# Normalisation stage of a four-layer image kernel: another order of its products, squares taken from PSUM, eight kept pieces spread out, the last three pieces left in SBUF

## The chip, the cores and the metric

The kernel runs on 1 core of one Trainium2 chip. The metric is the device time of one execution in microseconds (us). The engines are named as in the profile: PE (TensorE matmul), PEld (its weight loads), DVE (VectorE), ACT (ScalarE), POOL (GpSimd), SP (SyncE, which here only issues transfers). SBUF is the working memory, PSUM the memory that PE writes its products to, DRAM the large memory outside.

## The reference, cut to what matters

An image `x` of 256 x 256 pixels with 128 channels goes through four layers, each of the form `x = x + layer(group_norm(x))`. Only the first layer is touched by the change: row attention over the image, with a layer norm in front and a bias that is shared by all rows.

```
def _L0_conv_ref(z, ln_scale, ln_bias, Wq, Wk, Wv, Wb, Wg, Wo):      # z = _gn(x)
    mu = jnp.mean(z, axis=-1, keepdims=True)
    var = jnp.mean(jnp.square(z - mu), axis=-1, keepdims=True)
    zn = (z - mu) * jax.lax.rsqrt(var + EPS) * ln_scale + ln_bias
    q, k, v = zn @ Wq, zn @ Wk, zn @ Wv        # 4 heads of 32
    bias = zn @ Wb
    g = jax.nn.sigmoid(zn @ Wg)
    scores = jnp.einsum('bijhd,bikhd->bijkh', q, k) * (1.0 / C ** 0.5)
    scores = scores + bias[:, None, :, :, :]
    a = jax.nn.softmax(scores, axis=-2)
    o = jnp.einsum('bijkh,bikhd->bijhd', a, v)
    return (g * o).reshape(b, n, n, H * C) @ Wo
```

The other three layers (a recurrence in the frequency plane, a triangle product, a convolution) follow, and take the time from about 1660 us to the end.

## The kernel before, in words

All data is 32-bit. The image is worked on in 32 pieces of 2048 pixels (1 MB, eight image rows each), and attention in 128 row pairs of 512 pixels (`rp`), four to a piece. Three stages matter here:

**Statistics** (`statistics`, 0 to about 126 us). Every piece is read once, pixels on partitions, to sum `x` and its squares for the group norm. The last seven pieces read, which are pieces 0 to 6, go to tiles of their own (`kept`) and stay in SBUF.

**Normalisation** (`attention`, about 132 to 445 us). The group norm and the centring of the layer norm are folded into one matrix `lc` and one column `cb`. For each piece `m`:

- `turn(m)`: sixteen PE transposes (`pt`) put channels on partitions; ACT copies the first half and DVE the second half into `xo`, and POOL issues its write to DRAM (`xT`). `load(m + 2)` reads a piece that was not kept from DRAM again (`xin`), issued by SP.
- `centre(m, b)` for both halves `b`: two products `zc` (L60), a DVE addition of `cb` into `zs`, and ACT's square `sq` of `zs`.
- `variance(m)`: four products `var` with weights of 32 columns, so that each fills one of four strips of 32 partitions; ACT's logarithm and exponential make `rs`, one over the standard deviation.
- `normalise(m)`: four products `pr` spread `rs` over all channels (each uses a strip of 32 rows of PE); DVE multiplies `zs` by them into `zn`; POOL applies scale and bias and issues the write to DRAM (`znT`).
- `pair_bias(m)`: four products `pbias` make the bias of the piece's pixels; DVE copies it (`bi`), and SP issues four writes to DRAM (`biasD`). `load_bias` reads it back in another layout (`bias`).

The order on the engines is the program's (`tc.keep_in_program_order`), and every engine works its queue in order. One turn of the loop is: `turn(m+1)`, `variance(m)`, first half of `centre(m+1)`, `normalise(m)`, `pair_bias(m-1)`, second half of `centre(m+1)`. Of PSUM's eight banks, six hold three wide buffers of two banks, which `pt`, `zc` and `pr` share in turn, and two hold two row buffers, which `var` and `pbias` share in turn. A write to a buffer waits until its last reader is done. The weights of the later layers (`later_weights`) and the first row transforms (`row_transforms`, tile `hs`) are SP transfers of this stage too.

**Attention** (`attend_bounded`, about 445 to 1660 us). Ahead of its loop stand the projections `q`, `k`, `g`, `v` of the first two row pairs, the transposes of the bias (`pbt`, copied to `bT`), and the scores `sc` of the first two rows. In one turn, for row pair `rp`: POOL's folds `ks`, scores of the next pair, DVE's addition of the bias (`e`), ACT's exponentials, the four projections of pair `rp + 2`, the products `nd` of the exponentials with `v`, and the output `px`. `zn` and `x` of a row pair are read from DRAM by `chunk`; those of pairs 0 and 1 were read early into `first`. A second way, `attend_any`, stands behind a test of the weights and isn't taken.

Of the kernel before, what the change touches and what calls it, by code (L numbers as in the profile page):

```python
# [9 lines left out]
F32 = mybir.dt.float32  # L10
AF = mybir.ActivationFunctionType
ALU = mybir.AluOpType
# [5 lines left out]
P = 128  # L18
N = 256
NPIX = N * N  # L20
NCH = NPIX // 512
NH, HD = 4, 32
KS = 7
HC = P // 2
LN_EPS = 1e-5
LN_EXP = "natural_log_exp_and_others"
# [4 lines left out]
class Kernel:  # L31
# [27 lines left out]
    def mm(self, out, lhsT, rhs, start=True, stop=True):  # L59
        return self.nc.tensor.matmul(out, lhsT, rhs, start=start, stop=stop)  # L60
# [144 lines left out]
    def statistics(self, wp, weights, HD_, kept, src):  # L205
# [3 lines left out]
        nc, I = self.nc, self.i  # L209
        V = nc.vector  # L210
        x = I["x"].rearrange("b h w c -> (b h w) c")
        NM, KEPT = NPIX // 2048, len(kept)
        mv = wp.tile([P, 2], F32, name="mvx")
        with ExitStack() as c:
            sp = c.enter_context(self.pool(name="sp", bufs=1))
# [21 lines left out]
                                    start=count[j] < 2, stop=count[j] >= 4 * NM - 2)  # L237
                            count[j] += 1

            order = list(range(KEPT, NM)) + list(range(KEPT))  # L240
            spectrum, made = None, 0
            for n, m in enumerate(order):
                if m < KEPT:
                    xin = kept[m]
                else:
                    xin = io.tile([P, 2, 1024], F32, name="xin", bufs=3)
                nc.sync.dma_start(xin, src(m))
                for b in range(2):
                    xs = io.tile([P, 1024], F32, name="xs")
                    pin(V.tensor_tensor)(xs.rearrange("p (t c) -> p t c", t=8), xin[:, b].rearrange("p (t c) -> p t c", t=8),  # L250
                                    sh.unsqueeze(1).to_broadcast([P, 8, P]), ALU.subtract)
                    sq = io.tile([P, 1024], F32, name="sqx")
                    pin(self.act)(sq, xs, AF.Square)

                    add_up(xs, last)
# [91 lines left out]
    def attention(self, wp, later, xT, x1T, znT, biasD, HD_, stats1, shift1):  # L347
# [5 lines left out]
        with ExitStack() as c:  # L353

            bias = wp.tile([P, 2, NH, N], F32, name="bias")
            first = tuple(wp.tile([P, 1024], F32, name=n) for n in ("zn0", "xr0"))
            c1 = c.enter_context(ExitStack())
            kp = c1.enter_context(self.pool(name="kp", bufs=1))

            kept = [kp.tile([P, 2, 1024], F32, name=f"kept{m}") for m in range(7)]  # L360
            mv, (w, (lns, lnb), wo, small) = self.statistics(wp, self.attention_weights(wp), HD_, kept, src)
            with self.pool(name="awq", bufs=2, space=PSUM) as ps0:
                ab, mg, _ = self.group_affine(wp, ps0, None, self.g4, "0", True, mv=mv)
# [11 lines left out]

            io = c1.enter_context(self.pool(name="a1", bufs=3))
            work = c1.enter_context(self.pool(name="a1w", bufs=3))
            ps = c1.enter_context(self.pool(name="a1s", bufs=3, space=PSUM))  # L380
# [4 lines left out]
            pin = lambda f: lambda *a, **k: tc.keep_in_program_order(f(*a, **k))  # L385
            mm, act, tt, ts, copy = pin(self.mm), pin(self.act), pin(V.tensor_tensor), pin(V.tensor_scalar_add), pin(V.tensor_copy)
            transpose, acopy = pin(nc.tensor.transpose), pin(nc.scalar.copy)
            xin, xo, zn, sq, zs, rs, var, spreads = dict(enumerate(kept)), {}, {}, {}, {}, {}, {}, {}
            wide = lambda name: ps.tile([P, 1024], F32, name=name, tag="w")
            row = lambda name: ps.tile([P, 512], F32, name=name, tag="r", bufs=2)  # L390

            def load(m):
                if m < NM and m not in xin:
                    xin[m] = io.tile([P, 2, 1024], F32, name="xin")
                    nc.sync.dma_start(xin[m], src(m))

            def turn(m):
                if m >= NM:
                    return
                load(m + 2)  # L400
                xo[m] = io.tile([P, 2, P, 8], F32, name="xo")
                for b in range(2):
                    pt = wide("pt").rearrange("c (t p) -> c t p", t=8)
                    for t in range(8):
                        transpose(pt[:, t], xin[m][:, b, t * P:(t + 1) * P], self.ident)
                    (copy if b else acopy)(xo[m][:, b], pt.rearrange("c t p -> c p t"))
                nc.gpsimd.dma_start(xT[:, m * 2048:(m + 1) * 2048], xo[m].rearrange("c b p t -> c (b p t)"))

            def centre(m, b):
                if m >= NM:  # L410
                    return
                zc = wide("zc")
                for k in range(2):
                    mm(zc[:, k * 512:(k + 1) * 512], lc, xo[m][:, b].rearrange("c p t -> c (p t)")[:, k * 512:(k + 1) * 512])
                zs[m, b] = work.tile([P, 1024], F32, name="zs")
                ts(zs[m, b], zc, cb)
                sq[m, b] = work.tile([P, 1024], F32, name="sq")
                act(sq[m, b], zs[m, b], AF.Square)

            def variance(m):  # L420
                var = row("var")
# [4 lines left out]
                act(rs[m], rs[m], AF.Exp, scale=-0.5)  # L426

            def normalise(m):
                zn[m] = io.tile([P, 2048], F32, name="zn")
                pr = [wide("pr") for _ in range(2)]  # L430
                for k in range(4):
                    mm(pr[k // 2][:, (k % 2) * 512:(k % 2 + 1) * 512], spread[32 * k:32 * k + 32], rs[m][32 * k:32 * k + 32])
                for b in range(2):
                    z = zn[m][:, b * 1024:(b + 1) * 1024]
                    tt(z, zs[m, b], pr[b], ALU.mult)
                    nc.gpsimd.tensor_scalar(z, z, lns, lnb, ALU.mult, ALU.add)
                nc.gpsimd.dma_start(znT[:, m * 2048:(m + 1) * 2048], zn[m])

            def pair_bias(m):
                if m < 0:  # L440
# [8 lines left out]
                    nc.sync.dma_start(biasD[:, s:s + 512], bi[32 * k:32 * k + NH])  # L449

            tc.keep_in_program_order(self.table(LN_EXP))
            for m in range(7, 9):
                load(m)
            turn(0)
            centre(0, 0)
            centre(0, 1)
            for m in range(NM):
                turn(m + 1)
                variance(m)
                centre(m + 1, 0)  # L460
                normalise(m)
                pair_bias(m - 1)
                centre(m + 1, 1)
                if m == 5:
                    self.later_weights(later)
                elif m == 12:
                    self.first_rows = self.row_transforms(later.tile([P, 2, HC], F32, name="hs0"), HD_, 0)
                elif m == NM - 4:
                    load_bias(0, 192)
                    nc.sync.dma_start(first[0], znT[:, :1024])  # L470
                    nc.sync.dma_start(first[1], xT[:, :1024])
                elif m == NM - 1:
                    load_bias(192, 240)
            pair_bias(NM - 1)
            load_bias(240, 256)
            c1.close()

            flag = nc.values_load(small[0:1, 0:1])
            self.last = {}
            with tc.If(flag > 0) as branch:  # L480
                self.attend_bounded(xT, x1T, znT, bias, first, w, wo, stats1, shift1)
            self.last = {}
            with branch.Else():
                self.attend_any(xT, x1T, znT, bias, w, wo, stats1, shift1)
            self.last = {}

    def bounded(self, wp, raws, w, wb, m32):
# [62 lines left out]
            V.tensor_copy(fl, top[:, 1:2])  # L550
            return fl

    def attend_bounded(self, xT, x1T, znT, bias, first, w, wo, stats1, shift1):


        nc, tc = self.nc, self.tc
# [1 line left out]
        with ExitStack() as c:  # L558
# [17 lines left out]
            pin = lambda f: lambda *a, **k: tc.keep_in_program_order(f(*a, **k))  # L576
            mm, act_t, act_i = pin(self.mm), pin(act), pin(self.act)
            tt, stt, add = pin(V.tensor_tensor), pin(V.scalar_tensor_tensor), pin(nc.gpsimd.tensor_tensor)
            loaded, t, e, es, ks, nd, dn, og, x1s = {0: first}, {}, {}, {}, {}, {}, {}, {}, {}

            def chunk(rp):
# [12 lines left out]
            def project(rp, nm):  # L594
                if rp >= N // 2:
                    return
                z = chunk(rp)[0]
                o = pj.tile([P, 4, P] if nm == "v" else [P, 512], F32, name="t" + nm)
                if nm == "v":
                    pv = ps.tile([P, 4, P], F32, name="ppv", tag="pj")  # L600
                    for ch in range(4):
# [2 lines left out]
                else:  # L604
# [7 lines left out]
                t[rp, nm] = o  # L612

            def score(i):

# [59 lines left out]
            def output(rp):  # L675
# [8 lines left out]
                mm(px, wo["f"], og[rp])  # L684
                stt(x1[:, s], px, 1.0, xr, ALU.mult, ALU.add, accum_out=stats1[:, 0, rp:rp + 1])
                if rp % 2 == 1:
                    nc.gpsimd.dma_start(x1T[:, (rp - 1) * 512:(rp + 1) * 512], x1)

            def squares(rp):
                if rp >= 0:  # L690
# [58 lines left out]
            output(rp)  # L749
            squares(rp)  # L750

    def attend_any(self, xT, x1T, znT, bias, w, wo, stats1, shift1):

        nc, tc = self.nc, self.tc
        with ExitStack() as c:
            io = c.enter_context(self.pool(name="a2", bufs=2))
            pj = c.enter_context(self.pool(name="a2w", bufs=2))
# [842 lines left out]
```

## Time and profile before

| what | us |
|---|---|
| three runs | 4891.92, 4894.64, 4895.0 |
| median | 4894.64 |
| the profiled execution's own time | 4892.94 |
| its span | 4891.1 |

| engine | busy us | share of the span |
|---|---|---|
| PE | 4713.9 | 96% |
| DVE | 3631.1 | 74% |
| ACT | 3327.7 | 68% |
| POOL | 1859.5 | 38% |

| group in the normalisation stage | mean of one, ns |
|---|---|
| DVE addition `zs<-zc`, 128x1024 | 1278 |
| DVE multiplication `zn<-zs,pr`, 128x1024 | 1211 |
| ACT square `sq<-zs`, 128x1024 | 1057 |
| ACT copy `xo<-pt`, 128x1024 | 994 |
| DVE copy `xo<-pt`, 128x1024 | 1225 |
| DVE copy `bi<-pbias`, 128x512 | 682 |
| POOL scale and bias `zn<-zn`, 128x1024 | 1191 |

The second table is the page's first part, the third is from the groups of instructions between 148.7 and 425.3 us. A row of the order of time begins with its start and its length in us; a bracket at its end tells how long the engine had been idle and what ended that. One 32-bit product is two MATMUL instructions, and rows of the same kind that follow each other are merged, with their count behind an x; the ends of matmuls are modelled, so their starts are the surer numbers.

### The profile page before, as it was taken

The numbers are of one execution on the slowest core, as the hardware profiler recorded it, in microseconds if no ns is written. First come the engines' busy times: TensorE is split into PE (matmuls) and PEld (weight loads), VectorE is DVE, ScalarE is ACT, GpSimd is POOL, SyncE is SP. The second block draws the span as 40 slices with busy tenths as digits, with TensorE's granted clock in tenths as the row PEclk, the third lists the DMA queues.
The fourth block names the chain that finished last, engine by engine and source line by source line (L and its number), as shares of the span: only waits on it lengthen the run. The fifth ranks groups of instructions, "written<-read, shape, count | busy, mean of one in ns | idle before, by whom it ended". The sixth has DMA issues, their size and how long they took to land.

```text
span 4891.1 us, 78322 instructions
## 1 busy us (share of the span) xinstructions
PE 4713.9 (96%) x30415; PEld 2672.1 (55%) x30415; DVE 3631.1 (74%) x4551; ACT 3327.7 (68%) x5009; POOL 1859.5 (38%) x1296
## 2 busy tenths in 40 slices
PE   8999999999999899999999997999999999999999
PEld 2444555555555433333333332269999943369999
DVE  6666777777777699999999996763443357789886
ACT  6445888888888799999999995543333367762110
POOL 0333555555555466666666664421001100000000
PEclk9999999999999999999999998999999999999999
DMA  8795222222222245555555555996876688854432
GB/s 300 279 337 211 83 83 87 83 83 85 81 87 83 86 94 134 131 134 133 131 133 133 131 131 144 333 328 224 276 246 226 220 333 326 326 204 166 142 123 70
DMA packets 223923, 848.77 MB, mean 174 GB/s; under 512 B 59351, under 2 KB 62701, under 8 KB 174245
## 3 DMA queue, kind: packets, MB, share of 16 engines
q1 hardware_dynamic: 146638, 505.57, 31.0%
q0 software_dynamic: 75616, 337.76, 23.6%
q8 instruction: 244, 4.00, 0.3%
q14 instruction: 129, 1.05, 0.1%
q10 hardware_dynamic: 1296, 0.40, 0.0%
HBM read 505.18 MB, written 271.32 MB: 159 GB/s over the span
## 4 chain that ended last, share of the span: by engine, by line
PE 59%; ACT 14%; DVE 10%; issue 5%; POOL 1%; DMA 1%; POOLq 0%; ACTq 0%; DVEq 0%
PE z L60 9%; PE m L60 8%; PE nd L60 7%; PE sc L60 6%; PE zc L60 5%; PE po L60 5%; PE ppq L60 3%; PE ppv L60 3%; PE pe L60 2%; PE px L60 2%; PE py L60 2%; PE ppk L60 2%; PE ppg L60 2%; ACT L905 2%; ACT x2q L54 2%
## 5 line engine op out<-in xcount | busy, mean ns | idle before, releaser
L576 DVE TENSOR_TENSOR e<-sc,bT 128x1024 f32<-128x1024 f32 x512 | 613.2, 1219 | 259.0 <-PE sc L60 256.0
L576 POOL TENSOR_TENSOR ks<-e 128x1024 f32<-128x1024 f32 x256 | 601.7, 2371 | 448.6 <-PE nd L60 430.7
L54 ACT ACTIVATE e<-e 128x1024 f32<-128x1024 f32 x512 | 538.8, 1052 | 38.5 <-DVE e L576 29.1
L1091 DVE TENSOR_TENSOR LR<-z,sg 128x512 f32<-128x512 f32 x256 | 268.5, 1049 | 362.5 <-ACT sg L54 362.5
L60 PE MATMUL m<-U,v 128*128 128x128 f32 x4608 | 514.8, 275 | 0.0
L60 PEld LDWEIGHTS m<-U,v 128*128 128x128 f32 x4608 | 514.6, 192 | 0.0
L60 PE MATMUL z<-wf,zt 128*128 128x128 f32 x4096 | 458.4, 275 | 2.1 <-DVE zn L1091 1.4
L60 PEld LDWEIGHTS z<-wf,zt 128*128 128x128 f32 x4096 | 458.0, 192 | 3.3 <-DVE zn L1091 2.2
L54 ACT ACTIVATE sg<-z 128x512 f32<-128x512 f32 x256 | 152.9, 597 | 307.3 <-PE z L60 307.3
L54 ACT ACTIVATE sq<-zs 128x1024 f32<-128x1024 f32 x192 | 202.4, 1054 | 192.4 <-DVE zs L385 156.1
L1223 POOL DMA_DIRECT2D prodD<-o x128 | 69.3, 542 | 616.7 <-ACT o L54 609.2
L60 PE MATMUL sc<-tq,tk 32*128 32x256 f32 x4096 | 298.4, 403 | 2.8 <-DVE e L576 1.9
L933 POOL TENSOR_TENSOR fs<-f 128x512 f32<-128x512 f32 x64 | 176.5, 2759 | 275.7 <-DVE f L930 256.2
L60 PEld LDWEIGHTS sc<-tq,tk 32*128 32x128 f32 x4096 | 187.3, 185 | 160.0 <-PE px L60 94.8
L60 PE MATMUL nd<-e,tv 128*32 128x256 f32 x4096 | 271.3, 382 | 2.5 <-DVE og L576 2.5
L54 ACT ACTIVATE dn<-dn 128x512 f32<-128x512 f32 x384 | 237.9, 619 | 8.0 <-DVE dn L576 3.9
L933 POOL TENSOR_TENSOR u<-t,tr 128x512 f32<-128x512 f32 x64 | 229.6, 3588 | 11.9 <-DVE tr L936 9.9
L933 POOL TENSOR_TENSOR t<-t,v 128x1024 f32<-128x1024 f32 x64 | 209.6, 3275 | 52.5 <-DVE t L930 51.8
L60 PE MATMUL po<-LR 128*128 128x256 f32 x1024 | 222.1, 379 | 7.0 <-DVE LR L1091 7.0
L1476 ACT COPY m4s<-m 128x512 f32<-128x512 f32 x32 | 18.7, 584 | 287.2 <-PE m L60 287.2
L60 PEld LDWEIGHTS po<-LR 128*128 128x128 f32 x1024 | 194.2, 190 | 34.0 <-DVE LR L1091 7.7
L1486 POOL DMA_DIRECT2D out_dram<-ys x32 | 37.0, 1156 | 423.9 <-DVE ys L1484 412.0
(377 smaller groups left out, 10670.7 us busy)
## 6 DMA issues: line engine op xcount, KB each, us to landing
zt<-znT SPq DMA_DIRECT2D x128, 1024.0 KB
znT<-zn POOLq DMA_DIRECT2D x64, 1024.0 KB, 5.1
xin<-x2T SPq DMA_DIRECT2D x64, 1024.0 KB
xin<-in_x_dram SPq DMA_DIRECT2D x50, 1024.0 KB
xr<-x3T SPq DMA_DIRECT2D x46, 768.0 KB
xT<-xo POOLq DMA_DIRECT2D x32, 1024.0 KB, 9.4
xr<-xT SPq DMA_DIRECT2D x64, 512.0 KB
zn<-znT SPq DMA_DIRECT2D x64, 512.0 KB
```

Source lines behind the costliest of these rows:

```text
L54: return self.nc.scalar.activation(out, in_, func, bias=bias, scale=scale, **kw)
L60: return self.nc.tensor.matmul(out, lhsT, rhs, start=start, stop=stop)
L576: pin = lambda f: lambda *a, **k: tc.keep_in_program_order(f(*a, **k))
L905: pin(nc.scalar.preload_act_table_set(want))
L933: pin(nc.gpsimd.tensor_tensor(out, a, b_, op))
L1091: pin = lambda f: lambda *a, **k: tc.keep_in_program_order(f(*a, **k))
L1223: nc.gpsimd.dma_start(prodD[g * CQ + d].rearrange("(p a j) -> p a j", p=P, a=2), o.rearrange("p a j b -> p a (j b)"))
L1476: nc.scalar.copy(m4, m[4])
L1486: nc.gpsimd.dma_start(out[row:row + 8].rearrange("r p t c -> p (r t) c"), ys.rearrange("p g k t c -> p (g k t) c"))
```

## The change

- **Order of the products.** A turn of the loop is now `variance(m)`, `centre(m+1)` with both halves, `normalise(m)`, `pair_bias(m-1)`, `turn(m+2)`. Two pieces are transposed ahead of the loop.
- **Squares.** ACT squares `zc + cb` straight from PSUM (`bias=cb`); DVE's addition comes after it in the program and writes into `zn`, which is then multiplied in place. `zs` goes.
- **Kept pieces.** Eight pieces, 0, 4, 8, ... 28, stay in SBUF instead of seven, 0 to 6. The other 24 are read again, three ahead, in buffers (`qp`) that stand in their own region.
- **Last three pieces.** `zn` and `xo` of pieces 29, 30 and 31 aren't written to DRAM; attention starts with their twelve row pairs (`turns`). The projections of the first three row pairs are made in the end of the normalisation stage, in the row buffers of PSUM (`project`), and kept in tiles (`early`) which the loop then uses for its own projections in turn. `first` goes.

```diff
-            kept = [kp.tile([P, 2, 1024], F32, name=f"kept{m}") for m in range(7)]
+            kept = {m: kp.tile([P, 2, 1024], F32, name=f"kept{m}") for m in range(0, 32, 4)}
...
+            zp = c.enter_context(self.pool(name="a0", bufs=3, side="right"))
+            yp = c.enter_context(self.pool(name="ay", bufs=4, side="right"))
+            qp = c.enter_context(self.pool(name="aq", bufs=3, side="right"))
...
             def turn(m):
                 if m >= NM:
                     return
-                load(m + 2)
-                xo[m] = io.tile([P, 2, P, 8], F32, name="xo")
+                xo[m] = zp.tile([P, 2, P, 8], F32, name="xo")
...
-                nc.gpsimd.dma_start(xT[:, m * 2048:(m + 1) * 2048], xo[m].rearrange("c b p t -> c (b p t)"))
+                if m not in kept:
+                    load()
+                if m < NM - HELD:
+                    nc.gpsimd.dma_start(xT[:, m * 2048:(m + 1) * 2048], xo[m].rearrange("c b p t -> c (b p t)"))

-            def centre(m, b):
+            def centre(m):
                 if m >= NM:
                     return
-                zc = wide("zc")
-                for k in range(2):
-                    mm(zc[:, k * 512:(k + 1) * 512], lc, xo[m][:, b].rearrange("c p t -> c (p t)")[:, k * 512:(k + 1) * 512])
-                zs[m, b] = work.tile([P, 1024], F32, name="zs")
-                ts(zs[m, b], zc, cb)
-                sq[m, b] = work.tile([P, 1024], F32, name="sq")
-                act(sq[m, b], zs[m, b], AF.Square)
+                zn[m] = yp.tile([P, 2048], F32, name="zn")
+                for b in range(2):
+                    zc = wide("zc")
+                    for k in range(2):
+                        mm(zc[:, k * 512:(k + 1) * 512], lc, xo[m][:, b].rearrange("c p t -> c (p t)")[:, k * 512:(k + 1) * 512])
+                    sq[m, b] = work.tile([P, 1024], F32, name="sq")
+                    act(sq[m, b], zc, AF.Square, bias=cb)
+                    ts(zn[m][:, b * 1024:(b + 1) * 1024], zc, cb)
...
-                    tt(z, zs[m, b], pr[b], ALU.mult)
+                    tt(z, z, pr[b], ALU.mult)
                     nc.gpsimd.tensor_scalar(z, z, lns, lnb, ALU.mult, ALU.add)
-                nc.gpsimd.dma_start(znT[:, m * 2048:(m + 1) * 2048], zn[m])
+                if m < NM - HELD:
+                    nc.gpsimd.dma_start(znT[:, m * 2048:(m + 1) * 2048], zn[m])
...
-            for m in range(7, 9):
-                load(m)
+            for _ in range(3):
+                load()
             turn(0)
-            centre(0, 0)
-            centre(0, 1)
+            turn(1)
+            centre(0)
+            early = {}
+
+            def project(n, names):
+                if n not in early:
+                    early[n] = qp.tile([P, 4, 512], F32, name="proj", tag="xin")
+                z = zn[NM - HELD][:, n * 512:(n + 1) * 512]
+                for nm in names:
+                    pp, o = row("pp" + nm), early[n][:, "qkvg".index(nm)]
...
             for m in range(NM):
-                turn(m + 1)
                 variance(m)
-                centre(m + 1, 0)
+                centre(m + 1)
+                if m == NM - 1:
+                    project(0, "qkvg")
                 normalise(m)
                 pair_bias(m - 1)
-                centre(m + 1, 1)
+                turn(m + 2)
...
-                    nc.sync.dma_start(first[0], znT[:, :1024])
-                    nc.sync.dma_start(first[1], xT[:, :1024])
...
+            project(1, "qkvg")
             pair_bias(NM - 1)
             load_bias(240, 256)
+            project(2, "qkvg")
...
+            turns = [*range(N // 2 - 4 * HELD, N // 2), *range(N // 2 - 4 * HELD)]
+
+            def chunk(n):
+
+                rp = turns[n]
+                if rp // 4 in held:
+                    return tuple(x[:, rp % 4 * 512:(rp % 4 + 1) * 512] for x in held[rp // 4])
...
             def project(rp, nm):
                 if rp >= N // 2:
                     return
+                done = rp in early
+                o = early[rp % len(early)][:, "qkvg".index(nm)]
+                if nm == "v":
+                    o = o.rearrange("p (a b) -> p a b", b=P)
+                t[rp, nm] = o
+                if done:
+                    return
```

`HELD` is 3. In the built program of the changed kernel DVE's addition of a half waits for ACT's square of the same half, and the second `pr` half waits for the addition of the first `zc` half of the piece after it.

More of the change, by code (lines that the diff above doesn't have):

```diff
@@ L23 @@
 KS = 7
+HELD = 3
 HC = P // 2
@@ L211, in statistics @@
         x = I["x"].rearrange("b h w c -> (b h w) c")
-        NM, KEPT = NPIX // 2048, len(kept)
+        NM = NPIX // 2048
         mv = wp.tile([P, 2], F32, name="mvx")
@@ L238, in add_up @@
                             count[j] += 1
-            order = list(range(KEPT, NM)) + list(range(KEPT))
+            order = [m for m in range(NM) if m not in kept] + sorted(kept)
             spectrum, made = None, 0
             for n, m in enumerate(order):
-                if m < KEPT:
+                if m in kept:
                     xin = kept[m]
@@ L355, in attention @@
             bias = wp.tile([P, 2, NH, N], F32, name="bias")
-            first = tuple(wp.tile([P, 1024], F32, name=n) for n in ("zn0", "xr0"))
             c1 = c.enter_context(ExitStack())
             kp = c1.enter_context(self.pool(name="kp", bufs=1))
-            kept = [kp.tile([P, 2, 1024], F32, name=f"kept{m}") for m in range(7)]
+            kept = {m: kp.tile([P, 2, 1024], F32, name=f"kept{m}") for m in range(0, 32, 4)}
             mv, (w, (lns, lnb), wo, small) = self.statistics(wp, self.attention_weights(wp), HD_, kept, src)
@@ L387, in attention, with load @@
             transpose, acopy = pin(nc.tensor.transpose), pin(nc.scalar.copy)
-            xin, xo, zn, sq, zs, rs, var, spreads = dict(enumerate(kept)), {}, {}, {}, {}, {}, {}, {}
+            xin, xo, zn, sq, rs = dict(kept), {}, {}, {}, {}
             wide = lambda name: ps.tile([P, 1024], F32, name=name, tag="w")
             row = lambda name: ps.tile([P, 512], F32, name=name, tag="r", bufs=2)
-            def load(m):
-                if m < NM and m not in xin:
-                    xin[m] = io.tile([P, 2, 1024], F32, name="xin")
+            again = [m for m in range(NM) if m not in kept]
+            def load():
+                if again:
+                    m = again.pop(0)
+                    xin[m] = qp.tile([P, 2, 1024], F32, name="xin")
                     nc.sync.dma_start(xin[m], src(m))
@@ L428, in normalise @@
             def normalise(m):
-                zn[m] = io.tile([P, 2048], F32, name="zn")
                 pr = [wide("pr") for _ in range(2)]
@@ L451, in attention @@
             tc.keep_in_program_order(self.table(LN_EXP))
-            for m in range(7, 9):
-                load(m)
+            for _ in range(3):
+                load()
             turn(0)
-            centre(0, 0)
-            centre(0, 1)
+            turn(1)
[8 more added lines that the diff above has]
+                    if nm == "v":
+                        for ch in range(4):
+                            mm(pp[:, ch * P:(ch + 1) * P], z[:, ch * P:(ch + 1) * P], w["v"])
+                    else:
+                        mm(pp, w[nm], z)
+                    if nm == "g":
+                        act(o, pp, AF.Exp, scale=-1.0)
+                    else:
+                        act(o, pp, AF.Identity)
             for m in range(NM):
-                turn(m + 1)
                 variance(m)
-                centre(m + 1, 0)
+                centre(m + 1)
+                if m == NM - 1:
+                    project(0, "qkvg")
                 normalise(m)
                 pair_bias(m - 1)
-                centre(m + 1, 1)
+                turn(m + 2)
                 if m == 5:
@@ L469, in attention @@
                     load_bias(0, 192)
-                    nc.sync.dma_start(first[0], znT[:, :1024])
-                    nc.sync.dma_start(first[1], xT[:, :1024])
                 elif m == NM - 1:
                     load_bias(192, 240)
+            project(1, "qkvg")
             pair_bias(NM - 1)
             load_bias(240, 256)
+            project(2, "qkvg")
             c1.close()
+            held = {m: (zn[m], xo[m].rearrange("c b p t -> c (b p t)")) for m in range(NM - HELD, NM)}
             flag = nc.values_load(small[0:1, 0:1])
@@ L480, in attention @@
             with tc.If(flag > 0) as branch:
-                self.attend_bounded(xT, x1T, znT, bias, first, w, wo, stats1, shift1)
+                self.attend_bounded(xT, x1T, znT, bias, held, early, w, wo, stats1, shift1)
             self.last = {}
             with branch.Else():
-                self.attend_any(xT, x1T, znT, bias, w, wo, stats1, shift1)
+                self.attend_any(xT, x1T, znT, bias, held, w, wo, stats1, shift1)
             self.last = {}
@@ L551, in bounded, with attend_bounded @@
             return fl
-    def attend_bounded(self, xT, x1T, znT, bias, first, w, wo, stats1, shift1):
+    def attend_bounded(self, xT, x1T, znT, bias, held, early, w, wo, stats1, shift1):
         nc, tc = self.nc, self.tc
@@ L578, in attend_bounded @@
             tt, stt, add = pin(V.tensor_tensor), pin(V.scalar_tensor_tensor), pin(nc.gpsimd.tensor_tensor)
-            loaded, t, e, es, ks, nd, dn, og, x1s = {0: first}, {}, {}, {}, {}, {}, {}, {}, {}
-            def chunk(rp):
+            loaded, t, e, es, ks, nd, dn, og, x1s = {}, {}, {}, {}, {}, {}, {}, {}, {}
+            turns = [*range(N // 2 - 4 * HELD, N // 2), *range(N // 2 - 4 * HELD)]
[3 more added lines that the diff above has]
+                    return tuple(x[:, rp % 4 * 512:(rp % 4 + 1) * 512] for x in held[rp // 4])
                 m = rp // 2
@@ L596, in project @@
                     return
+                done = rp in early
+                o = early[rp % len(early)][:, "qkvg".index(nm)]
+                if nm == "v":
+                    o = o.rearrange("p (a b) -> p a b", b=P)
+                t[rp, nm] = o
+                if done:
+                    return
                 z = chunk(rp)[0]
-                o = pj.tile([P, 4, P] if nm == "v" else [P, 512], F32, name="t" + nm)
                 if nm == "v":
@@ L611, in project @@
                         act_i(o, pp, AF.Identity)
-                t[rp, nm] = o
             def score(i):
@@ L686, in output @@
                 if rp % 2 == 1:
-                    nc.gpsimd.dma_start(x1T[:, (rp - 1) * 512:(rp + 1) * 512], x1)
+                    nc.gpsimd.dma_start(x1T[:, (turns[rp] - 1) * 512:(turns[rp] + 1) * 512], x1)
             def squares(rp):
@@ L750, in attend_bounded, with attend_any @@
             squares(rp)
-    def attend_any(self, xT, x1T, znT, bias, w, wo, stats1, shift1):
+    def attend_any(self, xT, x1T, znT, bias, held, w, wo, stats1, shift1):
         nc, tc = self.nc, self.tc
+        for m, (zn, xo) in held.items():
+            nc.sync.dma_start(znT[:, m * 2048:(m + 1) * 2048], zn)
+            nc.sync.dma_start(xT[:, m * 2048:(m + 1) * 2048], xo)
         with ExitStack() as c:
```

## The prediction

> **What bounds the kernel now.** I read the page's slices first: TensorE (PE) is busy in nine tenths or more of nearly every slice, so only a view of one stage can say what a change in it is worth. The order of time from 131 us to 480 us shows one piece of the normalisation stage, over and over, and each starts 9.54 us after the one before: the var product of piece 1 starts at 148.70 and that of piece 30 at 425.31, 29 pieces later. One steady piece:
>
> ```profile
> 291.57 1.06 ACT L54 ACTIVATE sq<-zs 128x1024 f32<-128x1024 f32 x1 [3.00 <-DVE zs L385]
> 291.76 1.97 PE L60 MATMUL var<-sq,mean 128*32 128x512 f32 x8
> 292.68 0.14 PEld L60 LDWEIGHTS var<-sq,mean 128*32 128x32 f32 x4 [0.77 <-ACT sq L54]
> 293.66 1.98 PE L60 MATMUL zc<-xo,lc 128*128 128x512 f32 x4
> 295.58 1.14 PE L60 MATMUL pr<-rs,spread 32*128 32x512 f32 x8
> 295.74 1.28 DVE L385 TENSOR_SCALAR zs<-zc,cb 128x1024 f32<-128x1024 f32 x1 [2.65 <-PE zc L60]
> 296.65 1.07 PE L60 MATMUL pbias<-zn,wb 128*32 128x512 f32 x8
> 297.64 1.98 PE L60 MATMUL zc<-xo,lc 128*128 128x512 f32 x4
> ```
>
> From start to start: first half of var 0.92 us, second half 0.98, first zc half 1.92, pr 1.07, pbias 0.99, second zc half 1.83, transposes pt 1.83 (299.47 to 301.30). The sum is 9.54, with no idle stretch: PE sets the stage's pace. var is dear because its second half can't start before the second square; pbias, with weights of the same 128x32 shape and four products as well, takes 0.99 where var takes 1.90.
>
> The transfers are near their limit too, but don't set the pace. From 200 to 420 us they moved 334 GB/s at nine tenths busy or more; yet pieces 1 to 6, which are not loaded again, took the same 9.54 us.
>
> The stage's opening and end:
>
> ```profile
> 132.36 1.94 PE L385 MATMUL pt<-ident,kept 128*128 128x128 f32 x16 [0.30 <-issue]
> 135.08 1.42 SPq L395 DMA_DIRECT2D xin<-in_x_dram  x3
> ```
>
> ```profile
> 442.08 3.08 PE L60 MATMUL pbias<-zn,wb 128*32 128x512 f32 x8 [1.67 <-POOL zn L436]
> 448.72 0.32 SPq L371 DMA_DIRECT2D bias<-biasD  x1
> 455.57 0.70 PE L60 MATMUL sc<-tq,tk 32*128 32x256 f32 x4 [0.44 <-DVE bT L709]
> ```
>
> The first reload of x leaves SP only at 135.08, behind the later stages' weights and the four row-transform loads; before, nobody needed it until 194 us. After that, attention is a chain of PE products at 9.5 us per pair of rows. The change leaves that loop's products as they are.
>
> **Part 1: the order of products.** The new order is var(m), both zc halves of m+1, pr(m), pbias(m-1), pt(m+2). Both squares are then old when var starts, so its four products can go side by side: 0.99 by the pbias row instead of 1.90. Four zc products in a row took 3.53 in the opening (134.53 to 138.06, into pt); into pr it is 0.09 more (1.92 against 1.83), so 3.62. But pr loses what var gains. Its second half takes the PSUM buffer of the first zc half, so it waits for that half's square and add: in the built program's order the DVE add waits for ACT's square of the same tile, and the second pr half waits for the add. So pr's halves go one after the other: 0.92 (a half group costs what var's first half does) plus 1.07. New sum: 0.99 + 3.62 + 0.92 + 1.07 + 0.99 + 1.83 = 9.42. The round trip gives the same: var 0.99, zc to its reader 2.08 (293.66 to 295.74), square 1.06, add 1.28, two hand-overs of 0.05, second pr half 1.07, pbias 0.99, pt 1.83 = 9.40. Behind the waiting add DVE queues two pr multiplications (2.34), bi (0.68) and a copy (1.23): 7.1 us of 9.4, and pt's second half, which waits for the first multiplication, finds it 0.2 us early. Reading PSUM instead of SBUF costs the square about nothing: 1.06 from SBUF here, 1.02 for ACT's zs from zc later. So a piece saves 0.12 us, bounds 0 to 0.33 (pr's halves overlapping by a third); 29 pieces save 3.5 us, bounds 0 to 9.6.
>
> [...]
>
> **Part 2: the kept pieces.** Pieces 0, 4, ... 28 stay, so piece 1 must be read again at once, and PE stands still for it: pt of piece 1 stands ahead of zc of piece 0 in PE's order. Without the wait it would start at 134.2 (132.36 + 1.83). The reload leaves SP at 135.08 as before; its queue position doesn't change.
>
> ```profile
> q1 hardware_dynamic: 288, 1.13, 91.4%
> ```
>
> That is what the load queue moved from 136 to 140 us: a little over one piece's 1.05 MB. The statistics stage's loads ended one by one, 2.56 us apart, so I take them as served in order: piece 1 is usable at 140.6. Bounds: 139.9, and 151, when the queue has moved all three pieces. Then pt to 142.4, zc to 146.0, second square to 147.4, and with one period less pbias, and 0.4 for the adds that the first pt half now waits for, var(1) starts at 156.2 instead of 148.70: 7.5 us lost. SP and POOL hold nothing else up: pieces 2 and 3 are needed at 154 and 163, and the queue has moved their bytes by 146 and 151; from there each load has three buffers of lead.
>
> PE's standing still has a second price:
>
> ```profile
> 440.00:443.00 3.00, 1.33 (x8) 0.14 (x4) 2.45 (x3) 0.00 (x0) 2.16 (x2) 1.00 0.00 0
> 443.00:446.00 3.00, 2.87 (x7) 0.67 (x6) 0.69 (x1) 0.00 (x0) 0.78 (x2) 0.55 0.55 224
> 460.00:464.00 4.00, 3.44 (x24) 1.96 (x26) 2.36 (x2) 2.80 (x3) 2.35 (x1) 0.55 0.00 0
> ```
>
> The column before the last two is the granted clock. After PE stood idle for half of 434 to 443 the clock fell to half for 3.4 us, and again from 460.4 to 467.2. A stop of 6.4 us (134.2 to 140.6) will do the same: 3.4 to 6.8 us at half speed lose 1.7 to 3.4; I take 2.5. Opening: +10 us, bounds +7 to +20.
>
> Spreading takes transfers down: per four pieces 11.7 MB in 37.7 us, 310 GB/s against 334 now. A kept piece more lets the statistics stage's last load start unthrottled: 0.4 us saved, bounds 0 to 1.
>
> **Part 3: the last three pieces.** Six writes of 1 MB, the two early half-megabyte reads and twelve of attention's half-megabyte reads go. All of them lie beside PE's work: worth nothing by themselves. The projections of the first three row pairs move into the tail. Period 30: 7.80 before, 7.5 now. Before, var(31) to the first score took 22.46 us (433.11 to 455.57), and to the first nd product 37.9 (471.00). Now the ring of two row buffers makes the projections wait for DVE and ACT: pbias(31) starts 13.4 us after var(31) (8.97 before), its copy ends at 15.4, the bias goes to DRAM and back in 4.9 (as 445.89 to about 450.8 did), and after transposes and copies the first score starts at 22.4: no gain. Then the third pair's projections (465.2 to 469.9) are missing from the loop's first turn. What is late next is POOL's second fold, which ended at 466.67, so at most 3.4 of 4.7 are won; a clock at half speed there may take half of that back. I take -1.8, bounds -4 to +2. Row pairs 116 to 127 come first now; that costs nothing in the loop.
>
> **Sum.** +10.0 - 3.5 - 0.3 - 1.8 - 0.4 = +4.0 us on the profiled execution's 4892.94 (span 4891.1): 4896.9, and I say 4897. The median of the runs stands 1.7 above that execution, so by it the same sum is 4898.6. A measurement of this kernel can tell about 0.2%, 9.8 us, from no change: 4884.9 to 4904.4 is "the same".
>
> **Rivals.**
> - Slower, the late first load. If the three reloads share the queue, piece 1 lands with the third at 151, not 140.6: +10.4, so 4907. It decides from a landing of about 148. Against it: the loads that ended one by one. 0.12.
> - Slower, var stays in two halves. If the four strips don't overlap, a piece costs 10.3: 29 x 0.91 = 26 more, 4923. Against it: pbias does it in 0.99. 0.07.
> - Faster, the round trip doesn't bind. If square, add and pr's first half are done early enough for pr to stay at 1.07, a piece takes 8.5: 29 x 0.92 = 27 less, 4870. Against it: the add's wait in the built order; transfers would then need 344 GB/s. 0.09.
> - The forecast, 0.72, with an own range of 4888 to 4906 from the bounds of its terms.
>
> The forecast's upper edge holds some time beyond 4904.4, so: faster 0.10, same 0.69, slower 0.21. Range 4886 to 4908: it takes in the late load.
>
> **What would show it.** In the changed profile: a var group that takes about 1 us; pieces 9.3 to 9.5 us apart; a PE wait near 134 to 141 for xin, with a granted clock near 0.5 after it; squares that end before the adds of the same tile begin; first score about 22 us after var(31). Pieces under 9.2 or over 9.6 us apart, or a first wait beyond 146, would make the prediction wrong.

## The result, and the profile after

The changed kernel takes 4902.62 us in the median of 14 runs, the kernel before 4894.01 us in 14 runs beside it: a ratio of 1.0018, with an interval of 1.0010 to 1.0025. It is 8.6 us slower: inside what the forecast called "the same" (4884.9 to 4904.4), but the interval leaves no change out, so the slowdown is real and small. The profiled execution took 4899.83 us (span 4897.9), 6.9 us more than that of before.

One steady piece, in order of time:

```profile
299.85 1.06 PE L61 MATMUL var<-sq,mean 128*32 128x512 f32 x8
...
300.84 3.70 PE L61 MATMUL zc<-xo,lc 128*128 128x512 f32 x8
...
302.86 1.11 ACT L55 ACTIVATE sq<-zc,cb 128x1024 f32<-128x1024 f32 x1 [0.54 <-PE zc L61]
...
304.07 1.28 DVE L388 TENSOR_SCALAR zn<-zc,cb 128x1024 f32<-128x1024 f32 x1 [2.58 <-issue]
...
304.47 2.06 PE L61 MATMUL pr<-rs,spread 32*128 32x512 f32 x8
...
305.41 0.30 PEld L61 LDWEIGHTS pr<-rs,spread 32*128 32x128 f32 x4 [0.64 <-DVE zn L388]
...
306.47 1.06 PE L61 MATMUL pbias<-zn,wb 128*32 128x512 f32 x8
...
307.46 1.96 PE L388 MATMUL pt<-ident,xin 128*128 128x128 f32 x16
...
309.36 1.06 PE L61 MATMUL var<-sq,mean 128*32 128x512 f32 x8
```

From start to start: var 0.99 (1.90 before), both zc halves 3.63, pr 2.00 (1.07 before), pbias 0.99, pt 1.90; together 9.51 us, where 9.54 was. The line to look at is that of PEld at 305.41: the weights of pr's second half wait for DVE, whose addition ended at 305.35, because it did not begin before the square of the same tile was done (302.86 + 1.11). What var gained (0.91), pr lost (0.93).

The opening, in order of time, then the load queue's part from 134 to 140 us and two stretches from 140 to 146 us (the granted clock stands before the last two columns):

```profile
131.86 1.94 PE L388 MATMUL pt<-ident,kept 128*128 128x128 f32 x16 [0.30 <-issue]
...
134.43 9.26 SPq L401 DMA_DIRECT2D xin<-in_x_dram  x4
...
139.85 3.44 PE L388 MATMUL pt<-ident,xin 128*128 128x128 f32 x16 [6.05 <-DMA xin<-in_x_dram]
...
143.13 3.60 PE L61 MATMUL zc<-xo,lc 128*128 128x512 f32 x8
...
157.29 1.07 PE L61 MATMUL var<-sq,mean 128*32 128x512 f32 x8
```

```profile
q1 hardware_dynamic: 474, 1.31, 70.7%
```

```profile
140.00:143.00 3.00, 3.00 (x15) 3.00 (x16) 0.00 (x0) 1.01 (x1) 0.00 (x0) 0.51 1.02 344
143.00:146.00 3.00, 3.00 (x10) 1.46 (x9) 1.23 (x1) 0.95 (x1) 0.54 (x1) 1.00 0.99 406
```

PE stood still for 6.05 us until piece 1 had landed, when the queue had moved 1.31 MB, a little over one piece: the first load was served first. Then the clock was at half, and the transposes took 3.44 us instead of 1.94. The var products of piece 1, the last line above, start at 157.29 instead of 148.70.

The end of the stage, on PE:

```profile
440.52 1.04 PE L61 MATMUL var<-sq,mean 128*32 128x512 f32 x8
...
458.58 0.38 PE L745 MATMUL pbt<-ident,bias 128*128 128x128 f32 x2
...
460.26 1.75 PE L745 MATMUL pbt<-ident,bias 128*128 128x128 f32 x14 [1.31 <-DMA bias<-biasD]
...
462.45 0.70 PE L61 MATMUL sc<-proj 32*128 32x256 f32 x4 [0.44 <-DVE bT L747]
...
483.21 1.02 PE L61 MATMUL px<-og,wo 128*128 128x512 f32 x2
```

and in the kernel before:

```profile
433.11 1.05 PE L60 MATMUL var<-sq,mean 128*32 128x512 f32 x4
...
477.61 1.02 PE L60 MATMUL px<-og,wo 128*128 128x512 f32 x2
```

After the change the transposes of the bias wait 1.31 us for the bias itself, which left late (its last products, pbias(31), start 13.4 us after var(31), 9.0 before); the first score comes 21.9 us after var(31) (440.52), against 22.46 before. The first output `px` comes 42.7 us after var(31), against 44.5.

### The profile page after: what moved, and what is told of

The parts are those of the page before. It is cut to its first block, busy times and chain, and to the rows that moved or that the text cites. A ratio compares the mean times of both kernels' runs of the same rounds, so it can differ in the third digit from the quotient of the medians.

```text
span 4897.9 us, 78226 instructions
## 1 busy us (share of the span) xinstructions
PE 4716.3 (96%) x30415; PEld 2682.4 (55%) x30415; DVE 3631.1 (74%) x4551; ACT 3334.3 (68%) x5009; POOL 1855.8 (38%) x1290
## 4 chain that ended last, share of the span: by engine, by line
PE 66%; ACT 14%; DVE 11%; issue 5%; DMA 2%; POOL 1%; SPq 1%; ACTq 0%; DVEq 0%; POOLq 0%
PE z L61 9%; PE m L61 8%; PE zc L61 7%; PE nd L61 7%; PE sc L61 6%; PE po L61 5%; PE ppq L61 3%; PE ppv L61 3%; PE pe L61 2%; PE px L61 2%; PE ppk L61 2%; PE ppg L61 2%; PE py L61 2%; PE pr L61 2%; ACT L946 2%
## 5 line engine op out<-in xcount | busy, mean ns | idle before, releaser
L61 PE MATMUL sc<-proj 32*128 32x256 f32 x4096 | 299.8, 403 | 3.2 <-DVE e L605 2.4
L61 PEld LDWEIGHTS sc<-proj 32*128 32x128 f32 x4096 | 188.1, 185 | 160.7 <-PE px L61 94.8
L61 PE MATMUL nd<-e,proj 128*32 128x256 f32 x4096 | 272.8, 384 | 2.6 <-DVE og L605 2.6
L61 PE MATMUL av<-y,ident 128*128 128x512 f32 x384 | 192.4, 610 | 4.0 <-DVE y L971 4.0
```

## The experiments

**The add before the square, which reads SBUF.** In the kernel after:

```diff
-                    act(sq[m, b], zc, AF.Square, bias=cb)
-                    ts(zn[m][:, b * 1024:(b + 1) * 1024], zc, cb)
+                    ts(zn[m][:, b * 1024:(b + 1) * 1024], zc, cb)
+                    act(sq[m, b], zn[m][:, b * 1024:(b + 1) * 1024], AF.Square)
```

> One thing is changed in the kernel after: DVE adds the bias out of PSUM first, and ACT squares the sum from SBUF. Theory (two readers of one PSUM tile in a row hold pr): the first zc tile is free after the add alone, 1.2 us earlier, so pr's second half no longer waits, pr takes 1.07 us instead of 1.99, and a piece takes 0.99 + 3.62 + 1.07 + 0.99 + 1.83 = 8.50 us instead of 9.51. Thirty pieces give 30 us: about 4872 us. Rival 1 (transfers are next): 8.5 us a piece needs 344 GB/s; if 334 GB/s, the most that the kernel before moved, is the limit, a piece takes 8.8 us and the whole 4880. Rival 2 (pr waits for something else, the order itself is what it costs): pieces stay 9.4 to 9.5 us apart, 4900 to 4903. The opening's wait near 134 to 140 us stays in every case.

Measured: 4877.2 us, ratio to the kernel before 0.9969 (0.9957 to 0.9981). Pieces are 8.59 us apart throughout (from 183.37 to 191.96, for one). In order of time:

```profile
306.70 1.28 DVE L388 TENSOR_SCALAR zn<-zc,cb 128x1024 f32<-128x1024 f32 x1 [1.65 <-issue]
...
308.02 1.06 ACT L55 ACTIVATE sq<-zn 128x1024 f32<-128x1024 f32 x1 [1.91 <-DVE zn L388]
...
308.25 1.14 PE L61 MATMUL pr<-rs,spread 32*128 32x512 f32 x8
...
309.32 1.06 PE L61 MATMUL pbias<-zn,wb 128*32 128x512 f32 x8
```

pr takes 1.07 us (308.25 to 309.32): the wait is gone, and with it 25 us of the whole. The 30 us expected were too many: a piece takes 8.59, not 8.50 (pt 1.90, not 1.83), which is 3 us over the stage, and the end of the stage gave back some 2: 44.8 us from var(31) to the first px instead of 42.7. The opening's wait is still there (5.72 us).

**Piece 1 kept.** In the kernel after:

```diff
-            kept = {... for m in range(0, 32, 4)}
+            kept = {... for m in (0, 1, 5, 9, 13, 17, 21, 25)}
```

> One thing is changed in the kernel after: the eight kept pieces are 0, 1, 5, 9, ... 25 instead of 0, 4, 8, ... 28, so that piece 1 need not be read again. Theory (the opening's loss is the load of piece 1): PE goes from pt of piece 0 to pt of piece 1 without a stop or half clock, zc starts at about 135.6 us instead of 143.1, and var(1) at about 149.7 instead of 157.3: 7.6 us less, about 4895. The period stays 9.51 us. Rival 1 (the loss is in the order of products, which must fill from piece 1 on): var(1) comes before 155 us by no more than the half clock's 1.6 us, 4900 to 4902. Rival 2 (the first load is only put off): piece 2 is then late, a wait of several us appears before its pt near 146 to 152, and the time stays at 4900 or more.

Measured: 4896.46 us, ratio 1.0007 (0.9998 to 1.0016). On PE:

```profile
131.35 3.69 PE L388 MATMUL pt<-ident,kept 128*128 128x128 f32 x32 [0.30 <-issue]
...
149.53 1.06 PE L61 MATMUL var<-sq,mean 128*32 128x512 f32 x8
```

PE goes through both transposes without a stop, zc starts at 135.26, var(1) at 149.53: 7.8 us earlier than in the kernel after, of which 0.5 is the earlier start of the stage. The period stays 9.51 us. The trace agrees with the theory; the whole time fell by 6.2 us, 1.4 less than expected, and this is within what its runs differ by (4892.15 to 4903.63).

**Both.** The two edits together.

> Both edits in the kernel after: pieces 0, 1, 5, ... 25 are kept, and the add comes before the square, which reads SBUF. Theory: the gains add up, 30 + 7.6 us, about 4865. Rival (transfers are next): with shorter pieces and fewer kept ones at the end the load queue falls behind, and pieces are 8.8 us or more apart: 4873 or more.

Measured: 4868.53 us, ratio 0.9950 (0.9937 to 0.9964). Pieces stay 8.59 us apart with 336 GB/s, and no load is late. It took 3.5 us more than expected: a piece again takes 8.59 us and not 8.50, and the end of the stage had grown to 45.8 us (see below).

**The order alone.** The kernel before, with its transfers, its seven kept pieces and its square from SBUF:

```diff
             turn(0)
+            turn(1)
             centre(0, 0)
             centre(0, 1)
             for m in range(NM):
-                turn(m + 1)
                 variance(m)
                 centre(m + 1, 0)
+                centre(m + 1, 1)
                 normalise(m)
                 pair_bias(m - 1)
-                centre(m + 1, 1)
+                turn(m + 2)
```

(and four buffers instead of three for `zs`, two for `sq`).

> The kernel before with the new order of products alone: var(m), both halves of zc(m+1), pr(m), pbias(m-1), pt(m+2). Pieces 0 to 6 stay kept, the square reads the sum from SBUF as before, and all transfers stay. Theory: nothing reads a zc tile but the add, so pr does not wait and pieces that need no load (1 to 6) are 8.5 us apart instead of 9.54. From there each piece moves 3.19 MB (334 GB/s times 9.54 us): if about 334 GB/s is the limit, the period goes back to 9.5 us and the kernel gains 6 to 7 us, 4887; if 375 GB/s can be had, the pieces stay 8.5 us apart and it gains 30 us, 4865. Rival (the order itself is what made pr wait): 9.4 to 9.5 us throughout, 4891 to 4894.

Measured: 4863.72 us, ratio 0.9941 (0.9928 to 0.9955): 30 us faster than the kernel before. From piece 1 on, pieces are 8.59 us apart, but for one that takes 8.72. The stretch from 200 to 400 us:

```profile
200.00:400.00 200.00, 200.00 (x1128) 89.23 (x1120) 153.27 (x141) 104.01 (x117) 81.24 (x93) 1.00 0.99 370
```

PE is never idle, and the transfers, all of those of before, moved 370 GB/s at a share of 0.99. In the same stretch the kernel before moved 338 GB/s at a share of 0.96 (334 from 200 to 420 us). So that was no limit, and the change's saving in transfers was not needed for the faster piece.

**The add before the square, both from PSUM.** In the kernel after:

```diff
-                    act(sq[m, b], zc, AF.Square, bias=cb)
                     ts(zn[m][:, b * 1024:(b + 1) * 1024], zc, cb)
+                    act(sq[m, b], zc, AF.Square, bias=cb)
```

> One thing is changed in the kernel after: the add stands before the square, but the square still reads PSUM (in the run with the add first, it read SBUF). Theory (what holds pr is that both ACT and DVE read one zc tile, one after the other, whichever is first): the tile is free after 1.28 + 1.11 us as in the kernel after, the square begins when the add of the same tile has ended, and pieces stay 9.4 to 9.6 us apart: 4898 to 4907 us. Rival (what counts is only that DVE's add came late; with the add first, pr is free whatever else reads the tile): 8.6 us a piece, about 4877.

Measured: 4899.0 us in one run, pieces 9.51 us apart. In order of time:

```profile
303.53 1.28 DVE L388 TENSOR_SCALAR zn<-zc,cb 128x1024 f32<-128x1024 f32 x1 [1.69 <-PE zc L61]
304.85 1.11 ACT L55 ACTIVATE sq<-zc,cb 128x1024 f32<-128x1024 f32 x1 [1.91 <-DVE zn L388]
305.08 2.06 PE L61 MATMUL pr<-rs,spread 32*128 32x512 f32 x8
```

The square begins when the addition has ended (304.81), and pr takes 2.00 again (305.08 to 307.08). It is not which reader comes first that counts here, but that there are two: with the add as the only reader pr took 1.07.

**zc of piece 0 before pt of piece 1.** In the kernel after:

```diff
             turn(0)
-            turn(1)
             centre(0)
+            turn(1)
```

> One thing is changed in the opening of the kernel after: the zc products of piece 0 stand before the transposes of piece 1, so PE has 3.6 us of work while piece 1 is being read. Theory (the loss is the wait for piece 1, and the half clock comes from the length of the stop): PE's stop before pt of piece 1 shrinks from 6 to some 2.3 us, the granted clock stays at 1.00 after it (pt 1.8 to 1.9 us instead of 3.4), and var(1) starts 5 to 6 us earlier, at 151 to 152 us instead of 157.3: about 4897. Rival (the opening costs what it costs because the order needs piece 1 turned before anything else can follow): var(1) moves by less than 2 us, about 4902.

Measured: 4896.96 us in one run. On PE:

```profile
140.81 1.94 PE L388 MATMUL pt<-ident,xin 128*128 128x128 f32 x16 [2.86 <-DMA xin<-in_x_dram]
```

The stop is 2.86 us, the clock stays at 1.00 (140 to 143 us), and var(1) starts at 152.05, 20.0 us after the first transpose instead of 25.4: the 5 to 6 us of the theory.

**Products that nobody reads, in the stop.** In the kernel after:

```diff
             turn(0)
+            filler = wide("busy")[:, :P]
+            for _ in range(40):
+                mm(filler, self.ident, self.cmat)
             turn(1)
```

> One thing is added to the kernel after: 40 products of 128x128 by 128x128, whose result nobody reads, between the transposes of pieces 0 and 1, some 6.1 us by the 0.153 us that one takes in the stage before; they fill the time in which PE stood still. Theory (besides the wait, the stop costs half a clock): the granted clock stays at 1.00, pt of piece 1 takes 1.8 to 1.9 us instead of 3.4, var(1) starts 1.4 to 1.7 us earlier, at about 155.7 us. Rival (pt of piece 1 is slow because the rest of the piece is still landing): it stays at 3.3 us or more and var(1) at 157.3 or later.

Measured: 4902.18 us in one run. The 40 products took 9.1 us and not 6.1: they are 80 instructions, and the 0.153 us came from a row that counts instructions, not products, so it was no price of a product (one took 0.22 here). They overran the landing of the piece. So var(1) came at 161.30, not 155.7, and that part of the expectation failed. What the run was for still shows:

```profile
136.46 9.10 PE L61 MATMUL busy<-cmat,ident 128*128 128x128 f32 x80
145.39 1.91 PE L388 MATMUL pt<-ident,xin 128*128 128x128 f32 x16
```

With PE kept at work, the clock was 1.00 (143 to 149 us) and pt of piece 1 took 1.91 us, and from its start to var(1) 15.91 us passed, against 17.44 (139.85 to 157.29) in the kernel after. The half clock cost 1.5 us. Since the filler ran until after the piece had landed, this run alone doesn't rule out that pt was slow because data was still landing. The run before does: there pt began as soon as piece 1 had landed, at a clock of 1.00, and took 1.94 us.

**The early projections taken out.** The kernel with both edits, with `done = False` in the loop's `project` and nothing projected in the end of the stage.

> The kernel with both edits, but the projections of the first three row pairs go back to where they stood in the kernel before: two pairs ahead of pbt, the third in the loop's first turn. The last three pieces still stay in SBUF. Theory (the early projections stand in front of pbias(31) on PE, so the bias goes to DRAM and back 6 us later, uncovered): from var(31) to the first px 41 to 43 us instead of 45.8, no wait of pbt for the bias, 4864 to 4866 us. Rival (the tail's length is set by the bias's round trip and the clock, wherever the projections stand): 45 to 46 us, 4868 to 4869.

Measured: 4865.47 us, ratio 0.9940 (0.9923 to 0.9957); from var(31) to the first px 42.3 us instead of 45.8. On PE, first with the early projections, then without:

```profile
421.46 1.06 PE L61 MATMUL pbias<-zn,wb 128*32 128x512 f32 x8
...
428.60 3.24 PE L745 MATMUL pbt<-ident,bias 128*128 128x128 f32 x14 [2.10 <-DMA bias<-biasD]
```

```profile
413.00 2.23 PE L61 MATMUL pbias<-zn,wb 128*32 128x512 f32 x8 [1.68 <-POOL zn L444]
...
422.49 1.91 PE L745 MATMUL pbt<-ident,bias 128*128 128x128 f32 x16
```

With them, the last pbias starts 13.2 us after var(31) (408.22), and pbt waits 2.10 us for the bias and then takes 3.24 us for 14 transposes at a clock below 1.00 (0.86 from 425 to 430 us, 0.79 from 430 to 435; the same 14 take 1.75 us in the kernel with the add first); without them, 6.9 us after (406.11), and nothing waits for the bias. Placed before pbias, the projections lengthen the one path that nothing covers. The whole time differs by 3.1 us, which these few runs cannot tell from none; the trace can.

**The order alone, with zc of piece 0 first.** The kernel of the order alone, with `turn(1)` after both `centre(0, b)`.

> The kernel before with the new order of products in the loop (as in the run with the order alone), but in the opening the zc products of piece 0 stand ahead of the transposes of piece 1, so that its squares are made beside those. Theory: the two waits of var(0) for its squares there (0.81 and 0.60 us) go, pt(0) to var(1) takes 16.4 us instead of 17.8, the period stays 8.59 us, and the kernel takes 1.4 us less than with the order alone, about 4862. Rival: pr of piece 0 then waits for the squares of piece 1 and takes back what var(0) gains: 17.8 us, 4864.

Measured: 4864.49 us, ratio 0.9945 (0.9931 to 0.9959). From the first pt to var(1) 16.5 us instead of 17.8, as the theory had it; the whole time can't be told from that of the order alone, as 1.3 us lie below what the runs can tell. The order alone, this one, and both edits without early projections are all some 29 us faster than the kernel before and can't be told apart.

## Why the prediction was right, step by step

The forecast's terms against the two traces:

| term | forecast, us | measured, us | from |
|---|---|---|---|
| statistics | -0.4 | -0.5 | first pt 131.86 against 132.36 |
| opening | +10.0 | +9.1 | first pt to var(1): 25.43 against 16.34 |
| order of products, 29 pieces | -3.5 | -0.9 | var(1) to var(30): 275.73 against 276.61 |
| period 30 | -0.3 | -0.3 | 7.50 against 7.80 |
| end of the stage | -1.8 | -1.8 | var(31) to the first px: 42.69 against 44.50 |
| after the first px | 0 | +1.2 | span +6.8, first px +5.6 |
| sum | +4.0 | +6.8 | |

So the sign, the places and "the same" came out, and the size was too small: the order gave 2.6 us less than was taken, the opening cost 0.9 less, and 1.2 stand outside the terms.

- **The opening** was right in place and size. Piece 1 was usable at 139.85, where 140.6 was said and 151 was the rival. Its parts were a little off and partly made up for each other: the half clock costs 1.5 us (filled stop), where 2.5 was taken and 1.7 was the lower bound. Keeping piece 1 takes 7.25 us out of the opening (25.43 to 18.18), so the wait alone is 5.7. The other 1.8 (18.18 against 16.34) remain with piece 1 kept. That they come from the new order, which turns piece 1 before it centres piece 0, is likely: in the kernel of the order alone, centring first took back 1.3. In the changed kernel with piece 1 kept it wasn't run.
- **The order** is the term that was mis-sized: 0.12 us a piece was forecast, 0.03 measured. The mechanism, pr's second half behind the square and the add, was right, and two runs show it from both sides. The round trip as measured is var 0.99, zc to its reader 2.02, square 1.11, hand-over 0.10, add 1.28, hand-over 0.06, second pr half 1.06, pbias 0.99, pt 1.90: 9.51 instead of 9.40.
- **What the order's sum missed.** By PE's own sum most of the missing 0.09 us is pt (0.07), for which the 1.83 of its old place after zc was taken; after pbias it takes 1.90, in the kernels with the shorter pieces as well, so this is no wait for the adds. Why it does is open. In the round trip the two hand-overs (0.06 more than said) and the square (0.05 more) add to it, and zc gives 0.06 back. The square takes 1.113 us in the mean, 1.057 before, so "costs about nothing" was too low. But the square changed in two ways, and PSUM need not be the one that costs: in the same profile ACT's copy `zs<-zc` in a later layer, also 128x1024 out of PSUM but with no column to add, takes 1.014 us. The prediction left out the column `cb`. A copy is not a square, and no run separates the two. One sum in the prediction is off as well: DVE's work in a piece is 6.8 us by its rows (two adds 2.56, then 2.34, 0.68 and 1.23), not 7.1, which changes no term.
- **The rival that did not happen, "the round trip doesn't bind",** had nearly the right price for another program: 8.5 us a piece against 8.59 measured as soon as the tile has one reader. The 344 GB/s held against it were no hurdle, and the prediction's sentence that the transfers are near their limit was wrong: the order alone moved 370. The change got the new order right and took its gain back with the square from PSUM.
- **The last three pieces** gave 1.8 us, as forecast. The path was as told (pbias(31) 13.4 us after var(31) in both, first score 21.9 where 22.4 was said), but with bounds of -4 to +2 the exact hit is luck. Beside the shorter piece they gave nothing: the kernel of the order alone, which has none of this, needs 41.0 us from var(31) to the first px, the kernel after 42.7, the one with both edits 45.8.
- **Statistics.** The first pt of the nine experiments lies between 131.35 and 134.69 us, so a term of 0.4 us can't be told there. The 1.2 us after the first px can't be assigned either.

In both orders of square and add the second reader of a tile starts 0.04 to 0.10 us after the first has ended: 304.07 after 303.97 and 305.73 after 305.69 in the kernel after, 304.85 after 304.81 with the add before the square and both from PSUM. The runs show that the two follow each other, not why; no run shows what would happen without the wait.

A stop of 6.05 us was followed by a clock of 0.51 (140 to 143 us, kernel after), one of 2.86 us by 1.00 (140 to 143 us, zc of piece 0 first), and with the stop filled it was 1.00 too (143 to 149 us). The ends of the stage show that the length of a single stop doesn't decide it: in the kernel before the clock was at 0.50 from 444 to 446 us, after stops of no more than 1.67 us. In the kernel with both edits a stop of 2.10 us was followed by 14 transposes that took 3.24 us (clock 0.86 from 425 to 430 us, 0.79 from 430 to 435), in the kernel with the add first one of 2.00 us by 14 that took 1.75 us, as in the kernel after at a clock of 1.00 (460 to 462 us). What does decide there, no run separates.

## What to carry to other kernels

When a reader is moved from SBUF to a PSUM tile that another engine reads too, count the two readers one after the other, as they ran here (the second started 0.04 to 0.10 us after the first had ended), and ask which product takes that buffer next; one such square cost 0.92 us a piece and some 25 us of the whole, and hid that the new order by itself is worth 30. When products are put in another order, walk each buffer from its last reader to its next writer and add up that round trip as well as PE's own work. Before spreading a set of kept tiles over a loop, ask which pieces are needed before any load can land, and keep those: here keeping piece 1 took 7 us out of the opening.

## What was not expected of the hardware

- The square of 128x1024 takes 1.113 us out of PSUM with a column to add and 1.057 out of SBUF without one, in the mean over 200 to 400 us. Out of PSUM and without a column, ACT's copy of the same shape takes 0.994 in the kernel before, so the column is the likelier cost; no run tries a square with one and not the other.
- The transfers of this stage, which looked full at 338 GB/s and a busy share of 0.96 (200 to 400 us), went to 370 GB/s at 0.99 as soon as PE asked for them sooner. A share near full was no proof of a limit.
- A stop of PE of 2.10 us was followed by 14 transposes in 3.24 us in one kernel, one of 2.00 us by 14 in 1.75 us in another (both in the end of the stage).
